# A four-layer graph kernel: TensorE's instructions in the last pipeline pinned to the order of the text, with a new order of the steps

## The chip, the cores and the metric

The kernel runs on one core of one Trainium2 chip. A core has five engines with a queue each: TensorE (PE in the profile, with its weight loads shown apart as PEld), VectorE (DVE), ScalarE (ACT), GpSimd (POOL) and SyncE (SP), which here only issues DMA transfers. Each takes its instructions in the order of its own list and waits for the others through semaphores. Every result of TensorE lands in PSUM, a small memory, and has to be read out by VectorE or ScalarE before that piece of PSUM can be written again.

The metric is the time of one execution in microseconds (us) on the device; the comparison uses the median over several executions.

## The reference

Sixteen graphs (B = 16) of 1024 nodes (N) with 128 features (D), fp32, and a 0/1 adjacency matrix for each. Four layers, each added to its input and normalised over the features. Cut to what matters:

```python
# layer 0: two batch norms over ALL graphs, so nothing behind them can start before every graph was read
w = masked_row_softmax(adj.T);  region = BN((w @ x) @ k1 + b1)
people = BN((w.T @ region) @ k2 + b2);  x = layernorm(x + people)
# layer 1: one score per node; softmax over axis 1 of the matrix
h = x @ W + b;  e = leaky(s1[:, None] + s2[None, :])       # s1 = h @ a1, s2 = h @ a2 + b_a
att = softmax(where(adj > 0, e, -9e15), axis=1);  x = layernorm(x + relu(att @ h))
# layers 2 and 3: scores are symmetric; only a_0 matters where adj is 0 or 1
s = leaky((x * a) @ x.T);  att = softmax(where(adj == 1, s, -9e15), axis=-1)
x = layernorm(x + att @ x)
```

## The kernel before

`fast_path` has two parts. The first (layer 0, up to about 384 us of the profile) streams all adjacency matrices once and builds the batch-norm sums; the change leaves it as it is. The second, from about 384 us on, is a software pipeline over the 16 graphs and holds all that is changed. C = 8 is the number of blocks of 128 nodes, H = 2 that of halves of 512, G = 2 that of groups of four blocks, A = 129 is D with a column of ones added, which gives the sums of the softmax.

For each graph b the class `Batch` holds the steps:

- residual 0: `load` (x and the saved layer-0 rows `people`, DMAs), `people_rows(g)` (four transposes on TensorE, L777, copied out by ScalarE), `add_people(g)` (four matmuls, L784; VectorE adds, L786 and L789, and collects layer-norm statistics, L722 and L723), then `Norm.apply`.
- layer 1: `transpose(g)` (L757), `scores1` (two matmuls, L804, and four exponentials on ScalarE into `u1`, `u2`), `values1` (eight matmuls, L816, read out by VectorE into `hn`, and the exponential `q`, L821), then `chunk1(c)` for eight chunks: loads of a strip of both matrices (L826, L834), the mask on ScalarE (L828), a check of symmetry on VectorE (L836), the weights `e1` in two passes on VectorE (L839, L842, some 1.2 us each), a reciprocal (L845), a scaling of `hn` on ScalarE (L846) and the two matmuls into `po` (L849). After chunk 7, `relu1` (ScalarE), `add_transposed(g)` (transposes L730) and `apply`.
- layers 2 and 3, the same code twice: `transpose(g)` with a copy and a scaled copy on ScalarE (L759, L761); `weights(c)`, a triangular strip of scores (matmuls into `pbig`, L869; VectorE L871 reads it out less the mask, L874 is the leaky slope; ScalarE L875 the exponential); `mirror(c)`, which transposes a strip's blocks into the other half of the matrix (L882, copied by ScalarE L884); `sum(c0, n)`, n times eight matmuls of 129 columns into `pacc` (L892), then VectorE's division and residual (L896 to L900) with statistics; `apply`; in layer 3 `store`.

`Norm.apply` is a short chain over three engines: GpSimd's power (L442, L443), one small VectorE instruction (L740) and eight ScalarE instructions, one for each block (L742).

fp32 matmuls appear in the trace as two records each; transposes as one.

What sets the order. The function builds a list of (time, step) pairs, sorts it, and calls the steps in that order; this is the order of the text. A "turn" is a unit of 1.0 of that time: one graph enters per turn, and each turn works on layer 1 of graph t, on layer 2 of t-1, and on layer 3 of t-2 and t-3. The steps of a stage are spread evenly between a start a and an end z:

```python
place(t, 0.04, 0.92, t, layer1)
place(t, 0.06, 0.44, t - 1, scores, 2, V_L2)
place(t, 0.56, 0.94, t - 1, sums_of, 2)
```

The text is not what runs. The kernel is written in a tile framework whose scheduler simulates the engines at build time and takes, for each engine, the ready instruction of the highest rank; so an instruction of the text can be moved before others on its own engine. It also allots the buffers: `ps_big` and `ps_acc` have three PSUM buffers each (`pbig`, `pacc`), `ps_sum` one (`po`); the loads of `adjt` and the weights `e1` have three buffers, those of `adjn` two, and `hn`, `u1`, `xt` and `e` one each.

Of the kernel before, what the change touches and what calls it, by code (L numbers as in the profile page):

```python
# [8 lines left out]
F32 = mybir.dt.float32  # L9
# [381 lines left out]
def fast_path(ctx, tc, x, adj, adjt, k1, k2, w1, vecs, b_w, b_a, out, bad):  # L391
# [312 lines left out]
    with tc.tile_pool(name="r_load", bufs=3) as loads, tc.tile_pool(name="r_rows", bufs=2) as rows, \  # L704
# [4 lines left out]

        class Norm:  # L710
# [14 lines left out]
            def add_transposed(self, src, xin, g):  # L725

                pt = ps_acc.tile([P, 4, P], F32, name="pacc")
                for k in range(4):
                    c = 4 * g + k
                    nc.tensor.transpose(pt[:, k, :], src[:, c * P:(c + 1) * P], ident)  # L730
                nc.vector.tensor_add(self.xl[:, 4 * g:4 * g + 4, :D], pt,
                                     xin[:, 4 * g:4 * g + 4, :D])
                for k in range(4):
                    self.collect(4 * g + k)
# [10 lines left out]
        class Batch:  # L745
            def __init__(self, b):
                self.b = b

            def transpose(self, xl, g, layer, by=None):

                if g == 0:
                    self.xt = work.tile([P, N], F32, name=f"xt{layer}_")
                    if by is not None:
                        self.xw = work.tile([P, N], F32, name=f"xw{layer}_")
                pt = ps_acc.tile([P, 512], F32, name="pacc")
                for k in range(4):
                    nc.tensor.transpose(pt[:, k * P:(k + 1) * P], xl[:, 4 * g + k, :D], ident)  # L757
                cols = slice(g * 512, (g + 1) * 512)
                nc.scalar.copy(self.xt[:, cols], pt)  # L759
                if by is not None:  # L760
                    nc.scalar.mul(self.xw[:, cols], pt, by)  # L761
# [12 lines left out]
            def people_rows(self, g):  # L774
                pt = ps_acc.tile([P, 512], F32, name="pacc")
                for k in range(4):
                    nc.tensor.transpose(pt[:, k * P:(k + 1) * P], self.g[:, 4 * g + k, :D], ident)  # L777
                nc.scalar.copy(self.gt[:, g * 512:(g + 1) * 512], pt)

            def add_people(self, g):  # L780
                pt = ps_acc.tile([P, 4, P], F32, name="pacc")
                for k in range(4):
                    c = 4 * g + k
                    nc.tensor.matmul(pt[:, k, :], self.gt[:, c * P:(c + 1) * P], wide["k12s"],  # L784
                                     start=True, stop=True)
                    nc.vector.scalar_tensor_tensor(self.x0[:, c, :], wide["c12s"],  # L786
                                                   self.g[:, c, D:A], self.x0[:, c, :], ALU.mult,
                                                   ALU.add)
                nc.vector.tensor_add(self.n0.xl[:, 4 * g:4 * g + 4, :D], pt,  # L789
                                     self.x0[:, 4 * g:4 * g + 4, :])  # L790
                for k in range(4):
                    self.n0.collect(4 * g + k)
# [4 lines left out]
            def scores1(self):  # L797
# [3 lines left out]
                for h in range(H):  # L801
                    cols = slice(h * 512, (h + 1) * 512)
                    pu = ps_big.tile([P, 512], F32, name="pbig")
                    nc.tensor.matmul(pu, wa1_rep, self.xt[:, cols], start=True, stop=True)  # L804
# [4 lines left out]
            def values1(self):  # L809
                self.hn = work.tile([P, C, A], F32, name="hn")  # L810
                for c0 in range(0, C, 3):
                    n = min(3, C - c0)
                    ph = ps_acc.tile([P, 3, A], F32, name="pacc")
                    for k in range(n):
                        c = c0 + k
                        nc.tensor.matmul(ph[:, k, :], self.xt[:, c * P:(c + 1) * P], w1_sb,  # L816
                                         start=True, stop=True)
# [4 lines left out]
                self.po = ps_sum.tile([P, N], F32, name="po")  # L822

            def chunk1(self, c):
# [10 lines left out]
                e = loads.tile([P, N], F32, name="e1")  # L835
# [10 lines left out]
                nc.scalar.mul(self.hn[:, c, :D], self.hn[:, c, :D], rs)  # L846
                for h in range(H):
                    cols = slice(h * 512, (h + 1) * 512)
                    nc.tensor.matmul(self.po[:, cols], self.hn[:, c, :D], e[:, cols],  # L849
# [12 lines left out]
            def weights(self, c, layer, v0):  # L862
                if c == 0:
                    self.e = work.tile([P, C, N], F32, name=f"e{layer}_")
                for a in range(c * P, N, 512):
# [3 lines left out]
                    nc.tensor.matmul(ps[:, :n], self.xw[:, c * P:(c + 1) * P], self.xt[:, cols],  # L869
# [7 lines left out]
            def mirror(self, c):  # L877
                for a in range(c + 1, C, 4):
                    n = min(4, C - a)
                    pt = ps_acc.tile([P, 4, P], F32, name="pacc")  # L880
                    for k in range(n):
                        nc.tensor.transpose(pt[:, k, :], self.e[:, c, (a + k) * P:(a + k + 1) * P],  # L882
                                            ident)
                    nc.scalar.copy(self.e[:, a:a + n, c * P:(c + 1) * P], pt[:, :n, :])  # L884

            def sum(self, c0, n, xl, layer):
                norm = self.norm
                po = ps_acc.tile([P, 3, A], F32, name="pacc")
                for k in range(n):
                    c = c0 + k  # L890
                    for m in range(C):
                        nc.tensor.matmul(po[:, k, :], self.e[:, m, c * P:(c + 1) * P], xl[:, m, :],  # L892
# [15 lines left out]
        def does(f, *a):  # L908
            return lambda: f(*a)

        def residual0(s):
            return [s.load, *[does(s.people_rows, g) for g in range(G)],
                    *[does(s.add_people, g) for g in range(G)],
                    lambda: s.n0.apply()]

        def layer1(s):
            return [*[lambda g=g: s.transpose(s.n0.xl, g, 1) for g in range(G)],
                    s.scores1, s.values1, *[does(s.chunk1, c) for c in range(C)], s.relu1,
                    *[lambda g=g: s.n1.add_transposed(s.ot, s.n0.xl, g) for g in range(G)],
                    lambda: s.n1.apply()]  # L920

        def scores(s, layer, v0):
            def begin():
                s.xin = s.n1.xl if layer == 2 else s.norm.xl
            return [begin, *[lambda g=g: s.transpose(s.xin, g, layer, vec[:, v0:v0 + 1])
                             for g in range(G)],
                    *[does(s.weights, c, layer, v0) for c in range(C)]]

        def mirrors(s):
            return [does(s.mirror, c) for c in range(C - 1)]  # L930

        def sums_of(s, layer):
            def begin():
                s.norm = Norm(layer)
            return [begin, *[lambda c=c: s.sum(c, min(3, C - c), s.xin, layer)
                             for c in range(0, C, 3)],
                    lambda: s.norm.apply()] + ([s.store] if layer == 3 else [])

        at_work = {}
        order = []  # L940

        def place(t, a, z, b, steps, *args):

            if 0 <= b < B:
                s = steps(at_work.setdefault(b, Batch(b)), *args)
                order.extend((t + a + (z - a) * k / len(s), f) for k, f in enumerate(s))


        for t in range(-1, B + 3):
            place(t, 0.04, 0.92, t, layer1)  # L950
            place(t, 0.06, 0.44, t - 1, scores, 2, V_L2)
            place(t, 0.24, 0.52, t - 1, mirrors)
            place(t, 0.56, 0.94, t - 1, sums_of, 2)
            place(t, 0.56, 0.94, t - 2, scores, 3, V_L3)
            place(t, 0.74, 1.02, t - 2, mirrors)
            place(t, 0.06, 0.44, t - 3, sums_of, 3)
            place(t, 0.30, 0.80, t + 1, residual0)
# [28 lines left out]
        nc.tensor.matmul(pt[:, :1], ones, count, start=True, stop=True)  # L986
# [51 lines left out]
```

## Time and profile before

| | |
|---|---|
| median of 4 runs | 1936.48 us (1935.09 to 1944.55) |
| the profiled execution, own time | 1937.93 us |
| its span, first to last instruction | 1936.1 us |
| mean granted TensorE clock | 0.924 of full |
| layer 0 and its moments | up to about 384 us |
| pipeline, first steady mark to last (twelve turns) | 601.92 to 1718.12 us, 93.0 us a turn |

How to read the profile. "Busy" is the time in which an engine has an instruction in work; the ends of matmuls are modelled. "Granted clock" is the share of its full clock that TensorE was given. In the timeline a row gives start, duration, engine, line of the code, operation, output and inputs and how many alike were merged; in square brackets stands the idle time of the engine ahead of it and the instruction that ended it. The steady marks of the table are the sums of layer 3 behind the transposes L757 in the chain of waits: they come back every 92.6 to 93.5 us.

### The profile page before, as it was taken

Reading aid. Unit: us, or ns where it says so; the run is one execution under the profiler, and the core shown is the slowest. Engines: PE = TensorE matmul, PEld = TensorE weight load, DVE = VectorE, ACT = ScalarE, POOL = GpSimd, SP = SyncE. Lnnn points to the kernel's source line nnn. Section 1 sums busy time; section 2 is a strip of 40 time slices with the busy share of each in tenths; the row PEclk is TensorE's granted clock in tenths of the full one; section 3 lists DMA queues with packets and bytes.
Section 4 is the critical chain, followed back from the end, with each engine's and each line's share of the span. In section 5 each row is a group of like instructions: output and inputs, shape, how many; then the busy total and the mean of one; then the engine's idle time right before and its main releaser. Section 6 shows DMA issues by size and latency. Waiting matters only on the chain.

```text
span 1936.1 us, 28354 instructions
## 1 busy us (share of the span) xinstructions
PE 1630.3 (84%) x10093; PEld 1298.4 (67%) x10093; DVE 1322.1 (68%) x3931; ACT 1027.5 (53%) x2161; POOL 137.1 (7%) x252
## 2 busy tenths in 40 slices
PE   6998999767888889797888888888888888888795
PEld 6988898734556666566666666666666657666684
DVE  4655555467796959595868777686868595958444
ACT  4534444236555555656565655556565555655533
POOL 0000000010100010110101010101000000000100
PEclk9999999869898989998989999898999898989888
DMA  8966664343350504041413232231414040402000
GB/s 295 321 238 248 242 223 159 107 143 91 122 158 8 163 12 158 21 148 34 136 51 119 72 98 92 78 110 59 136 34 149 20 157 13 147 1 74 11 1 25
DMA packets 110969, 216.53 MB, mean 112 GB/s; under 512 B 7776, under 2 KB 63712, under 8 KB 110816
## 3 DMA queue, kind: packets, MB, share of 16 engines
q1 hardware_dynamic: 108512, 206.08, 32.4%
q10 hardware_dynamic: 2304, 8.52, 1.1%
q8 instruction: 82, 1.34, 0.3%
q14 instruction: 71, 0.58, 0.1%
HBM read 197.67 MB, written 16.91 MB: 111 GB/s over the span
## 4 chain that ended last, share of the span: by engine, by line
PE 58%; DVE 14%; ACT 13%; DMA 9%; POOL 3%; issue 2%; SPq 0%; DVEq 0%; ACTq 0%
PE pacc L892 21%; PE pbig L869 8%; PE po L849 8%; PE pb L543 5%; DMA at<-in_adj_dram 5%; PE pz L506 4%; DMA adjt<-in_adjt_dram 3%; PE pacc L757 3%; PE pacc L882 2%; DVE e L839 2%; PE pbig L804 2%; PE pacc L816 1%; DVE ln_st L722 1%; ACT m L499 1%; ACT pen L828 1%
## 5 line engine op out<-in xcount | busy, mean ns | idle before, releaser
L849 PE MATMUL po<-e,hn 128*128 128x512 f32 x512 | 270.6, 661 | 78.2 <-ACT hn L846 77.8
L849 PEld LDWEIGHTS po<-e,hn 128*128 128x128 f32 x512 | 97.5, 207 | 190.1 <-ACT hn L846 108.8
L896 DVE TENSOR_SCALAR sums<-pacc 128x3 f32<-128x3 f32 (+1 forms) x96 | 15.4, 160 | 283.7 <-PE pacc L892 283.4
L543 PE MATMUL pb<-v,m 128*128 128x258 f32 x1024 | 156.0, 294 | 22.2 <-DVE g L548 21.9
L506 PE MATMUL pz<-x,m 128*128 128x258 f32 x1024 | 163.1, 301 | 7.0 <-ACT m L499 3.2
L828 ACT ACTIVATE pen<-adjt,minus_root 128x1024 fp8e5<-128x1024 int32 x128 | 147.2, 1150 | 38.9 <-DMA adjt<-in_adjt_dram 38.6
L839 DVE SCALAR_TENSOR_TENSOR e<-u,q,u 128x1024 f32<-128x1024 f32 x128 | 162.4, 1279 | 0.8 <-ACT q L821 0.8
L543 PEld LDWEIGHTS pb<-v,m 128*128 128x128 f32 x1024 | 137.9, 197 | 26.8 <-DVE g L548 24.3
L842 DVE SCALAR_TENSOR_TENSOR e<-e,adjt 128x1024 f32<-128x1024 f32 x128 | 154.8, 1220 | 0.0
L506 PEld LDWEIGHTS pz<-x,m 128*128 128x128 f32 x1024 | 139.9, 199 | 10.3 <-ACT m L499 4.7
L836 DVE SCALAR_TENSOR_TENSOR e<-adjn,adjt 128x1024 f32<-128x1024 int32 (+7 forms) x128 | 95.6, 749 | 14.4 <-PE po L849 12.6
L846 ACT ACTIVATE hn<-hn,rs 128x128 f32<-128x128 f32 x128 | 50.8, 402 | 80.3 <-DVE rs L845 75.8
L499 ACT CAST m<-at 128x1024 fp32r<-128x1024 int32 x64 | 66.0, 1048 | 44.3 <-DMA at<-in_adj_dram 44.3
L548 DVE TENSOR_TENSOR g<-pb,lo 128x129 f32<-128x129 f32 x128 | 36.0, 289 | 72.2 <-ACT lo L547 72.0
L509 DVE TENSOR_TENSOR z<-pz,lo 128x128 f32<-128x128 f32 x128 | 35.7, 288 | 66.4 <-ACT lo L508 66.1
L547 ACT COPY lo<-pb 128x129 f32<-128x129 f32 x128 | 33.1, 269 | 69.4 <-PE pb L543 67.4
L508 ACT COPY lo<-pz 128x129 f32<-128x129 f32 x128 | 33.1, 269 | 66.0 <-PE pz L506 65.8
L501 DVE CAST m<-at 128x1024 fp32r<-128x1024 int32 x64 | 44.1, 689 | 21.2 <-DMA at<-in_adj_dram 21.0
L536 PE MATMUL moments<-reg 128*128 128x130 f32 x256 | 48.6, 277 | 0.0
L551 PE MATMUL moments<-g 128*128 128x130 f32 x256 | 48.4, 274 | 0.0
L786 DVE SCALAR_TENSOR_TENSOR x<-c12s,g,x 128x128 f32<-128x128 f32 x128 | 39.0, 343 | 0.1
L551 PEld LDWEIGHTS moments<-g 128*128 128x128 f32 x256 | 39.0, 190 | 0.0
(1265 smaller groups left out, 4020.7 us busy)
## 6 DMA issues: line engine op xcount, KB each, us to landing
at<-in_adj_dram SPq DMA_DIRECT2D x128, 512.0 KB, 5.6
adjt<-in_adjt_dram SPq DMA_DIRECT2D x128, 512.0 KB, 4.2
people<-g ACTq DMA_DIRECT2D x16, 520.0 KB, 7.3
g<-people SPq DMA_DIRECT2D x16, 520.0 KB, 3.6
xf<-in_x_dram SPq DMA_DIRECT2D x16, 512.0 KB, 4.3
adjn<-in_adj_dram SPq DMA_DIRECT2D x16, 512.0 KB, 4.7
x<-in_x_dram SPq DMA_DIRECT2D x16, 512.0 KB, 5.5
adjn<-in_adj_dram SPq DMA_DIRECT2D x16, 448.0 KB, 4.7
```

Of the source, the lines that this page charges most:

```text
L499: nc.scalar.copy(self.m[:, i, :], at)
L506: nc.tensor.matmul(pz[:, :2 * A], self.m[:, i, c * P:(c + 1) * P], self.x2[:, i, :], start=(i == 0), stop=(i == C - 1))
L543: nc.tensor.matmul(pz[:, :2 * A], self.m[:, j, c * P:(c + 1) * P], self.v2[:, j].rearrange("p s a -> p (s a)"), start=(j == 0), stop=(j == ...
L551: nc.tensor.matmul(moments2[:, :A + 1], self.g[:, c, :D], self.g[:, c, :], start=(self.b == 0 and c == 0), stop=(self.b == B - 1 and c == ...
L757: nc.tensor.transpose(pt[:, k * P:(k + 1) * P], xl[:, 4 * g + k, :D], ident)
L828: nc.scalar.activation(self.pen[:, c, :], at, AF.Square, bias=minus_root, scale=BIG_ROOT, saturate=False, accum_out=checks[:, self.b, c:c ...
L836: nc.vector.scalar_tensor_tensor(e[:, :n], an[:, :n], 1.0, at[:, c * P:], ALU.mult, ALU.not_equal, accum_out=unlike[:, self.b, c:c + 1])
L839: nc.vector.scalar_tensor_tensor(e, self.u2, self.q[:, c:c + 1], self.u1, ALU.mult, ALU.max)
L842: nc.vector.scalar_tensor_tensor(e, e, 1.0, at, ALU.mult, ALU.mult, accum_out=total)
L849: nc.tensor.matmul(self.po[:, cols], self.hn[:, c, :D], e[:, cols], start=(c == 0), stop=(c == C - 1))
L869: nc.tensor.matmul(ps[:, :n], self.xw[:, c * P:(c + 1) * P], self.xt[:, cols], start=True, stop=True)
L892: nc.tensor.matmul(po[:, k, :], self.e[:, m, c * P:(c + 1) * P], xl[:, m, :], start=(m == 0), stop=(m == C - 1))
```

## The change

Three things, all in the pipeline and its `Norm`.

1. Every matmul and transpose of the pipeline goes through a small wrapper that calls `tc.keep_in_program_order`: the scheduler may not move it ahead of the TensorE instruction that stands before it in the text. The other engines' instructions are still ordered by the scheduler.
2. `chunk1` is cut in two: `weights1(c)` (loads, mask, weights, scaling of `hn`) and `sum1(c)` (the two matmuls into `po`), so that they can stand at different places of the text. `po` is allotted at the first sum instead of in `values1`.
3. The list of times is rewritten for each step by hand, with `weights1` of chunk c at 0.12 + 0.095 c and its `sum1` at 0.21 + 0.095 c of the turn, `mirror` about 0.11 behind the strip it reads, the sums of layers 2 and 3 at 0.44, 0.55 and 0.66 behind that layer's start, and so on.

No arithmetic is added or removed, and no buffer count changes.

```diff
+        def matmul(*args, **kwargs):
+            tc.keep_in_program_order(nc.tensor.matmul(*args, **kwargs))
+
+        def transpose(*args):
+            tc.keep_in_program_order(nc.tensor.transpose(*args))
...
-            def transpose(self, xl, g, layer, by=None):
+                self.e1 = {}
+
+            def transposed(self, xl, g, layer, by=None):
...
-                self.po = ps_sum.tile([P, N], F32, name="po")
-
-            def chunk1(self, c):
+
+            def weights1(self, c):
...
-                e = loads.tile([P, N], F32, name="e1")
+                e = self.e1[c] = loads.tile([P, N], F32, name="e1")
...
+
+            def sum1(self, c):
+                if c == 0:
+                    self.po = ps_sum.tile([P, N], F32, name="po")
                 for h in range(H):
                     cols = slice(h * 512, (h + 1) * 512)
-                    nc.tensor.matmul(self.po[:, cols], self.hn[:, c, :D], e[:, cols],
+                    matmul(self.po[:, cols], self.hn[:, c, :D], self.e1[c][:, cols],
                                      start=(c == 0), stop=(c == C - 1))
...
-        for t in range(-1, B + 3):
-            place(t, 0.04, 0.92, t, layer1)
-            place(t, 0.06, 0.44, t - 1, scores, 2, V_L2)
-            place(t, 0.24, 0.52, t - 1, mirrors)
-            place(t, 0.56, 0.94, t - 1, sums_of, 2)
-            place(t, 0.56, 0.94, t - 2, scores, 3, V_L3)
-            place(t, 0.74, 1.02, t - 2, mirrors)
-            place(t, 0.06, 0.44, t - 3, sums_of, 3)
-            place(t, 0.30, 0.80, t + 1, residual0)
+        for b in range(B):
+            s = Batch(b)
+            place(b - 0.80, s.load)
+            for g in range(G):
+                place(b - 0.68 + 0.02 * g, s.people_rows, g)
+                place(b - 0.60 + 0.03 * g, s.add_people, g)
+                place(b + 0.02 + 0.02 * g, lambda s=s, g=g: s.transposed(s.n0.xl, g, 1))
+                place(b + 0.94 + 0.02 * g,
+                      lambda s=s, g=g: s.n1.add_transposed(s.ot, s.n0.xl, g))
+            place(b - 0.54, lambda s=s: s.n0.apply())
+            place(b + 0.07, s.scores1)
+            place(b + 0.09, s.values1)
+            for c in range(C):
+                place(b + 0.12 + 0.095 * c, s.weights1, c)
+                place(b + 0.21 + 0.095 * c, s.sum1, c)
+            place(b + 0.90, s.relu1)
+            place(b + 0.97, lambda s=s: s.n1.apply())
+            for layer, v0, at in ((2, V_L2, b + 1.08), (3, V_L3, b + 2.53)):
+                place(at, norm_of, s, layer)
+                for g in range(G):
+                    place(at + 0.01 + 0.02 * g,
+                          lambda s=s, g=g, l=layer, v=v0: s.transposed(s.xin, g, l, vec[:, v:v + 1]))
+                for c in range(C):
+                    place(at + 0.06 + 0.035 * c, s.weights, c, layer, v0)
+                for c in range(C - 1):
+                    place(at + 0.17 + 0.04 * c, s.mirror, c)
+                for k, c in enumerate(range(0, C, 3)):
+                    place(at + 0.44 + 0.11 * k,
+                          lambda s=s, c=c, l=layer: s.sum(c, min(3, C - c), s.xin, l))
+                place(at + 0.75, lambda s=s: s.norm.apply())
+            place(b + 3.35, s.store)
```

In the built program the TensorE lists differ as the change says. Before, the eight `po` pairs of a turn stand close together, the fourth to the sixth with one or two other rows of the list between them; after, they stand five to twelve rows apart over the whole turn. The lists of VectorE and ScalarE, which the scheduler makes, differ too.

## The prediction

> **What bounds the kernel now.** I read the page first, then the windows of a steady turn, then TensorE's timeline of that turn and its clock.
>
> ```profile
> PE 1630.3 (84%) x10093; PEld 1298.4 (67%) x10093; DVE 1322.1 (68%) x3931; ACT 1027.5 (53%) x2161; POOL 137.1 (7%) x252
> ...
> PE 58%; DVE 14%; ACT 13%; DMA 9%; POOL 3%; issue 2%; SPq 0%; DVEq 0%; ACTq 0%
> ```
>
> The second line is the chain of waits by engine: TensorE leads, but over 40% of the span the chain runs elsewhere. The turn from 830 us, all engines (PE, PEld, DVE, ACT, POOL, then clock, DMA share, GB/s):
>
> ```profile
> 830.00:923.00 93.00, 79.40 (x469) 60.65 (x468) 68.72 (x208) 53.57 (x110) 7.98 (x12) 0.93 0.28 89
> ```
>
> TensorE is idle for 13.6 of 93.0 us, VectorE for 24.3. TensorE's timeline shows where:
>
> ```profile
> 871.70 0.44 PE L882 MATMUL pacc<-ident,e__8094 128*128 128x128 f32 x2 [2.91 <-ACT e__8094 L875]
> 877.48 0.48 PE L882 MATMUL pacc<-ident,e__8094 128*128 128x128 f32 x1 [5.34 <-ACT e__8094 L875]
> ...
> 880.31 6.85 PE L892 MATMUL pacc<-xl__7201,e__8094 128*128 128x129 f32 x48
> ...
> 890.98 5.52 PE L892 MATMUL pacc<-xl__7201,e__8094 128*128 128x129 f32 x48
> ...
> 916.70 3.32 PE L849 MATMUL po<-e,hn 128*128 128x512 f32 x4 [4.51 <-ACT hn L846]
> ...
> 921.19 1.88 PE L849 MATMUL po<-e,hn 128*128 128x512 f32 x4
> ```
>
> Three gaps (2.91, 5.34, 4.51) make 12.8 of the 13.6 us. The reader should also see their echo: the same 48 sums take 6.85 us behind a gap and 5.52 later; the same two matmuls of `po` 3.32 and 1.88. The granted clock in windows of 2 us explains it:
>
> ```profile
> 876.00:878.00 2.00, 0.52 (x3) 0.50 0.00 0
> ...
> 880.00:882.00 2.00, 2.00 (x11) 0.50 0.04 8
> ```
>
> The clock is halved from about 877.5 to 883 and from 916.7 to 920.3, which costs half of 9.1 us, 4.5. So a turn is 93.0 = work at full clock + 13.6 + 4.5, the work being 74.9. From rows at full clock: sums 256 records at 0.112 (5.36 us for 48 from start to start) 28.6; `po` 32 at 0.43 13.8; scores 9216 columns in two passes at 0.43 for 512, 15.5; 96 transposes at 0.11, 10.6; L804, L816, L784 5.3. Sum 73.8; the missing 1.1 I keep as 1.5% of friction.
>
> The long gaps come from the layer norm, which ScalarE's queue puts ahead of exponentials TensorE needs:
>
> ```profile
> 870.11 0.20 POOL L442 TENSOR_SCALAR rs_t<-ln_mv__8116 128x8 f32<-128x8 f32 x1
> ...
> 870.39 1.81 POOL L443 TENSOR_TENSOR ln_rstd__8311<-rs_t,neg_half 128x8 f32<-128x8 f32 x1
> ...
> 873.86 3.17 ACT L742 ACTIVATE xl__8114<-xl__8114,ln_off__8315,ln_rstd__8311 128x128 f32<-128x128 f32 x8
> ```
>
> From VectorE's last statistic it takes 2.1 us on GpSimd, 0.2 on VectorE and 3.1 on ScalarE.
>
> **The change, part by part.** The wrapper and the split of `chunk1` add no instruction: their own cost is nothing, since the same 73.8 us of TensorE, 69 of VectorE and 54 of ScalarE remain. What they change is who stands ahead of whom, so I followed one turn of the new lists, engine by engine, with durations from rows. VectorE's rows overlap: an L839 at 902.77 lasts 1.28 but its successor starts at 903.96, so it counts 1.19. The clock starts with VectorE's first L839 of a graph, which waits for `q`.
>
> A. VectorE, up to the reciprocal of chunk 5. Now layer 2's strips stand between the chunks: seven L839 at 1.19 (8.3), six L842 at 1.22 (7.3), layer 2's L871 and L874 (4608 columns each at 0.60 for 512, 10.8), four L836 (2.4), L769 (1.2), two L789 (1.2), ten pairs of statistics (2.9), some twenty small ones (2.0). 36.1 us, and 1.6 of waiting for GpSimd in the norm of residual 0, which has 0.5 us of other VectorE work in front. TensorE has only 27.7 us of work in this stretch and loses ten us in gaps: 1.4 (`po` of chunk 1 for L846), 1.8 (a PSUM buffer that ScalarE reads late behind eight L742), 4.3, 1.7 and 0.8. The 4.3 is `po` of chunk 3: ScalarE has the mask L828 of another chunk ahead of its scaling L846, and that chunk's strip is loaded only when VectorE's L842 frees the buffer. SP's queue has the 520 KB of `people` just ahead of it; in the turn shown a strip issued at 924.33 reached its mask at 929.47, 5.1 us. Behind that `po` stand layer 2's sums, and for them waits the norm of layer 2. It ends at 37.7.
>
> B. Scaling of chunk 5 on ScalarE, and behind it the copies L759 and L761 of layer 3: 0.2 + 0.4 + 0.6 + 0.7. At 39.6 TensorE starts layer 3's scores.
>
> C. TensorE without a gap to the end of layer 2's last sum: 3840 columns of scores 6.4, two chunks of `po` 3.4, 80 records of sums 9.0, 13 transposes 1.4. 20.2, to 59.8. VectorE has 18 us in the stretch and keeps up.
>
> D. From that sum to the relu: VectorE's division and statistics 2.2, GpSimd 2.1, L740 0.2, then on ScalarE eight L742 (3.1), with three copies and two exponentials (2.0) ahead of the relu (0.6). 10.2, to 70.0. TensorE has 7 us of other work there and stands 2.9. What is late next are the transposes of the relu.
>
> E. From the relu to the copy of the next graph's layer-1 rows: transposes and L731 1.9, statistics 2.4, GpSimd 2.1, L740 0.2, eight L742 3.1, copy 0.6, in all 10.3, to 80.3. TensorE has 7.3 of sums and transposes and stands 3.0: this copy is behind the eight L742 in ScalarE's queue, though it does not need them.
>
> F. TensorE to the next graph's first strip: L804 1.7, 48 records of sums 5.4, transposes 0.9, L816 1.8, one L869 0.9, and 0.8 of waiting for ScalarE; `q` 0.2. 11.7, to 92.0.
>
> Sum: 36.1 + 1.6 + 1.9 + 20.2 + 10.2 + 10.3 + 11.7 = 92.0 at full clock. It leaves TensorE idle for 18 us (less its work of 73.8) instead of 13.6, with 4.3 instead of 5.34 as the largest gap.
>
> What this leaves out: friction of 1.5% on the 32 us of TensorE on the path, 0.5; VectorE's seams in A, where windows of 10 us filled by it show 9.7 busy, 0 to 1.1, taken 0.6; and the clock. For gaps near 3 us the nearest row is one at the pipeline's start:
>
> ```profile
> 428.00 2.74 PE L849 MATMUL po<-e,hn 128*128 128x512 f32 x4 [2.58 <-ACT hn L846]
> ```
>
> Those four records take 1.88 at full clock: 0.9 lost behind a gap of 2.58 us. So each of the gaps of 4.3, 2.9 and 3.0 may cost between 0 and the 2.7 us lost behind 5.34; behind the first, TensorE's 1.7 us of slack takes part; behind the second, the chain of E runs on other engines. I take 1.2, 0.3 and 0.2: 1.7 together, bounds 0 and 3.5.
>
> The Trainium skill, "TensorE: Matmul & The Clock Gate", Part 1, says the clock is halved after an idle window of about 3.4 us that runs freely, and advises no gaps above some 3 us. By that rule only the 4.3 us gap would cost anything and the clock term would be 1.2; by the row above, where 2.58 us were enough, it is the 1.7 I take.
>
> A turn is then 92.0 + 0.5 + 0.6 + 1.7 = 94.8 against 93.0, bounds 92.5 and 97.1. Thirteen such turns lie between the second and the fifteenth graph: 13 x 1.8 = 23 us. I cost the fill and the drain of the pipeline at nothing: at both ends there is little to interleave, and the chains (eight chunks of 3.7 us on VectorE at the start; scores, sums, norm of the last graph at the end) do not change; bounds -10 and +10. The profiled execution took 1937.93, so 1961; the median lies 1.5 below it: 1960.
>
> **The rivals.**
>
> Faster. The layer-1 chunks now spread over the turn, and VectorE's 24 idle us are there to be used. If the relu and the copy in D and E come before the L742 that I put ahead of them, TensorE has no gap after B: 39.6 + (73.8 - 27.7) = 85.7, with friction and seams 87. That is -6 a turn, 13 x -6 = -78, 1858. For it: a norm's eight L742 and TensorE's sums are of like length, so a us of error in the chain moves it. Against: ScalarE's list is fixed as I read it. It decides from the point where the two gaps in D and E, 5.9 us in my sum, fall under 3 together.
>
> Much slower. The load of part A is the rule, not one case: each strip waits for L842, the mask for the strip, and `po` for what stands behind the mask in ScalarE's queue; pinned, nothing passes it on TensorE. With two more gaps of 2 us on the path, 98.7 a turn: 13 x 5.7 = 74, 2010. For it: SP's list now mixes `people`, x and the strips. Against: ten turns of before show only 14 us of L828 waiting for its strip, and spreading the chunks gives the loads more time.
>
> Nothing to see. Gaps change places and the sum stays: 92.3 to 93.7 a turn, 1927 to 1946. That the pinning does nothing at all I exclude: the TensorE lists of the two programs differ.
>
> **How the numbers follow.** About 0.5% (10 us) is what a measurement of this kernel can tell; three of the four runs agree within 2 us, one lies 8 above. Forecast (93.7 to 97.5 a turn) 0.45, 1946 to 1995, likeliest 1960; much slower 0.15; nothing to see 0.12; faster 0.28. So slower 0.60, same 0.12, faster 0.28. The range leaves out half of the faster case and a third of the much slower one, together 0.19: 1885 to 2005.
>
> **What would show it.** In the profile of the changed kernel: a steady turn of 94 to 95 us; TensorE's busy time about unchanged, with more but shorter gaps; a gap of about 4 us at a `po` in the first half of a turn, ended by the scaling L846 that stands behind a mask in ScalarE's queue; gaps of about 3 us at the transposes of the relu and at the matmuls of `scores1`, both ended by ScalarE; the large VectorE wait of before (13.5 us for a sum) cut up. Wrong I am if a turn comes in below 92 us, and then the step to look at is D or E; if A runs longer than 39 us, the step is the loads.

## The result, and the profile after

| | before | after |
|---|---|---|
| median | 1937.98 us (1927.64 to 1944.75, 78 runs) | 1941.59 us (1929.34 to 1950.1, 52 runs) |
| ratio to before, 95% interval | | 1.002 (1.0011 to 1.0028) |
| profiled execution: span | 1936.1 us | 1942.2 us |
| of it, from the pipeline's first transposes to the end | 1545.9 us | 1547.8 us |
| steady turn, mean of eleven | 93.0 us | 92.9 us |
| mean granted clock | 0.924 | 0.942 |

The change makes the kernel 0.2% slower: the interval excludes 1, but the step is below the 0.5% that the prediction took as the least a measurement can tell. The steady turns are counted between the relu's transposes of the fourth and of the fifteenth graph. The fourth row counts from the transposes of `people` of the first graph, where the unchanged layer 0 ends. That point lay between 383.2 and 397.0 us in the fourteen profiled executions of this study, with the same code ahead of it, so profiles are compared from there.

In the lines of after the two wrapped calls have one line each, L713 for every matmul and L716 for every transpose; they are told apart by their tiles. L847 and L850 are the two passes of VectorE over the weights of layer 1, L854 ScalarE's scaling of `hn`, L836 the mask, L750 the layer norm's last pass, L768 and L770 the copies of transposed rows, L868 the relu, L887 the exponential, L896 the copy of a mirrored block.

The page of after: the engines' busy times, and the chain of waits by engine.

```profile
PE 1639.2 (84%) x10093; PEld 1302.9 (67%) x10093; DVE 1328.5 (68%) x3931; ACT 1021.0 (53%) x2161; POOL 152.7 (8%) x252
...
PE 46%; DVE 24%; ACT 13%; DMA 8%; POOL 6%; issue 2%; SPq 0%; DVEq 0%; ACTq 0%
```

The busy times are those of before within 1%, but for GpSimd's (152.7 us for 137.1). The chain has moved: VectorE has 24% of it instead of 14%, TensorE 46% instead of 58%. The same stretch of 93 us as before, by the windows view:

```profile
830.00:923.00 93.00, 79.41 (x468) 59.98 (x467) 69.70 (x209) 53.31 (x112) 9.19 (x12) 0.96 0.27 87
```

TensorE is idle for 13.6 us of it, to a tenth what it was. Where it stands idle is new. TensorE's timeline of after, one turn:

```profile
838.55 3.19 PE L713 MATMUL po<-e,hn 128*128 128x512 f32 x4 [3.80 <-ACT hn L854]
841.53 6.05 PE L713 MATMUL pacc<-xl__7512,e__7721 128*128 128x129 f32 x48
...
849.28 1.98 PE L713 MATMUL pbig<-xt__8048,xw__8049 128*128 128x512 f32 x4 [0.83 <-ACT xw__8049 L770]
...
876.95 0.33 PE L716 MATMUL pacc<-ident,e__8064 128*128 128x128 f32 x1 [0.89 <-ACT e__8064 L887]
879.91 1.78 PE L716 MATMUL pacc<-ident,u 128*128 128x128 f32 x8 [2.62 <-ACT u L868]
881.48 6.53 PE L713 MATMUL pacc<-xl__6890,e__8064 128*128 128x129 f32 x48
...
890.53 1.98 PE L713 MATMUL pbig<-xt__8390,wa_rep 128*128 128x512 f32 x4 [1.65 <-ACT xt__8390 L768]
```

The gaps of 5.34 and 2.91 us at the mirror transposes are gone. In their place stand 3.80 at the `po` pair of chunk 3, 2.62 at the transposes of the relu, 1.65 at `scores1` and several smaller ones, all ended by ScalarE. The echo of the slow clock is still there: the pair of `po` 3.19 us, the 48 sums behind it 6.05, and 6.53 behind the relu.

ScalarE's timeline of after shows why chunk 3's `po` is late:

```profile
836.96 1.15 ACT L836 ACTIVATE pen<-adjt,minus_root 128x1024 fp8e5<-128x1024 int32 x1 [1.91 <-DMA adjt<-in_adjt_dram]
...
838.11 0.39 ACT L854 ACTIVATE hn<-hn,rs 128x128 f32<-128x128 f32 x1
```

The mask of another chunk waits 1.91 us for its strip, and the scaling that `po` needs stands behind it.

### The profile page after: what moved, and what is told of

It is laid out like the page before. It is cut to its first block, busy times and chain, and to the rows that moved or that the text cites. A ratio compares the mean times of both kernels' runs of the same rounds, so it can differ in the third digit from the quotient of the medians.

```text
span 1942.2 us, 28298 instructions
## 1 busy us (share of the span) xinstructions
PE 1639.2 (84%) x10093; PEld 1302.9 (67%) x10093; DVE 1328.5 (68%) x3931; ACT 1021.0 (53%) x2161; POOL 152.7 (8%) x252
## 4 chain that ended last, share of the span: by engine, by line
PE 46%; DVE 24%; ACT 13%; DMA 8%; POOL 6%; issue 2%; SPq 0%; DVEq 0%; ACTq 0%
PE pacc L713 18%; PE pbig L713 7%; PE pb L543 6%; PE po L713 5%; DMA at<-in_adj_dram 5%; DVE e L847 4%; PE pz L506 4%; PE pacc L716 4%; DVE e L850 4%; DMA adjt<-in_adjt_dram 2%; DVE ln_st L730 2%; POOL rs_t L442 1%; ACT m L499 1%; DVE e L844 1%; PE moments L536 1%
## 5 line engine op out<-in xcount | busy, mean ns | idle before, releaser
L713 PE MATMUL po<-e,hn 128*128 128x512 f32 x512 | 272.2, 659 | 82.9 <-ACT hn L854 82.9
L713 PEld LDWEIGHTS po<-e,hn 128*128 128x128 f32 x512 | 97.7, 204 | 175.3 <-ACT hn L854 96.4
L836 ACT ACTIVATE pen<-adjt,minus_root 128x1024 fp8e5<-128x1024 int32 x128 | 146.6, 1150 | 49.5 <-DMA adjt<-in_adjt_dram 48.8
L847 DVE SCALAR_TENSOR_TENSOR e<-u,q,u 128x1024 f32<-128x1024 f32 x128 | 163.6, 1279 | 9.6 <-ACT q L830 9.5
L850 DVE SCALAR_TENSOR_TENSOR e<-e,adjt 128x1024 f32<-128x1024 f32 x128 | 155.5, 1216 | 0.0
L908 DVE TENSOR_SCALAR sums<-pacc 128x3 f32<-128x3 f32 (+1 forms) x96 | 15.3, 159 | 201.6 <-PE pacc L713 200.6
L854 ACT ACTIVATE hn<-hn,rs 128x128 f32<-128x128 f32 x128 | 51.5, 403 | 106.1 <-DVE rs L853 106.0
L716 PE MATMUL pacc<-ident,u 128*128 128x128 f32 x128 | 27.7, 387 | 43.2 <-ACT u L868 43.2
L716 PEld LDWEIGHTS pacc<-ident,u 128*128 128x128 f32 x128 | 21.2, 196 | 47.9 <-ACT u L868 47.5
```

Of the source, the lines that this page charges most:

```text
L713: tc.keep_in_program_order(nc.tensor.matmul(*args, **kwargs))
L716: tc.keep_in_program_order(nc.tensor.transpose(*args))
L836: nc.scalar.activation(self.pen[:, c, :], at, AF.Square, bias=minus_root, scale=BIG_ROOT, saturate=False, accum_out=checks[:, self.b, c:c ...
L847: nc.vector.scalar_tensor_tensor(e, self.u2, self.q[:, c:c + 1], self.u1, ALU.mult, ALU.max)
L850: nc.vector.scalar_tensor_tensor(e, e, 1.0, at, ALU.mult, ALU.mult, accum_out=total)
```

## The experiments

Twelve kernels. All times of a row come from that kernel; the ratio is to before on the same chip. "Pipeline" and "turn" are the profiled execution's, counted as in the table above.

| kernel | ratio to before (95%) | pipeline, us | turn, us |
|---|---|---|---|
| before | 1 | 1545.9 | 93.0 |
| after | 1.002 (1.0011 to 1.0028) | 1547.8 | 92.9 |
| e1_pin_only: old text, pinned | 1.0584 (1.0554 to 1.0615) | 1656.5 | 100.2 |
| e2_order_only: new text, not pinned | 0.9843 (0.9816 to 0.987) | 1517.9 | 91.7 |
| e3_warm | 0.9984 (0.9967 to 1.0001) | 1543.1 | 92.5 |
| e9_warm_both | 1.0301 (1.0268 to 1.0333) | 1599.6 | 96.8 |
| e12_warm_big | 1.0013 (0.9993 to 1.0033) | 1544.4 | 92.4 |
| e6_apply_late | 0.9859 (0.9807 to 0.9911) | 1518.3 | 91.4 |
| e7_sum_later | 0.9828 (0.977 to 0.9886) | 1508.4 | 90.2 |
| e4_early_layer1 | 0.9595 (0.9573 to 0.9618) | 1464.0 | 87.4 |
| e5_early_unpinned | 0.9452 (0.9405 to 0.9499) | 1430.2 | 85.1 |
| e8_both_moves | 0.9411 (0.9361 to 0.9461) | 1437.1 | 85.6 |
| e11_moves_later | 0.9748 (0.9706 to 0.9791) | 1492.4 | 89.3 |
| e10_moves_unpinned | 0.9155 (0.9114 to 0.9196) | 1386.2 | 82.1 |

### The two halves of the change

e1 puts the wrapper into the kernel before and leaves its text alone; e2 takes it out of the changed kernel.

```diff
 # e1, in the kernel before
-    nc.tensor.transpose(pt[:, k, :], ...)
+    transpose(pt[:, k, :], ...)          # and so for all matmuls of the pipeline
 # e2, in the changed kernel
-    tc.keep_in_program_order(nc.tensor.matmul(*args, **kwargs))
+    nc.tensor.matmul(*args, **kwargs)    # and so for transpose
```

> The kernel before, its order of the text untouched, with TensorE's instructions of the pipeline pinned to it; nothing else of the change. Theory W (a turn is the chain that I walked: VectorE's, ScalarE's and GpSimd's queues in series with stretches of TensorE; TensorE's own gaps and its slow clock lie beside it) has the sums of a chunk directly behind the chunk's weights in this text, so pinned TensorE waits for the whole of each chunk with everything else behind it: slower, 97 to 102 us a turn, 1990 to 2055. Rival N (pinning and placing both do next to nothing, and the result near zero is the sum of two nothings): 1930 to 1948.

> The changed kernel with the pinning taken away: the same steps at the same places of the text, TensorE's instructions free again for the scheduler. Theory W: the scheduler brings TensorE's work ahead where it finds it ready, the chain over VectorE's waits for q stays, 92 to 94 us a turn, 1925 to 1950. Rival G (pinning costs and the new places gain, and they cancelled): under 1915 here, as much faster as the pinning alone is slower. Rival N: 1930 to 1948.

Measured: the pin alone costs 5.8%, the new text alone wins 1.6%. In pipeline us the pin costs 111 with the old text and 30 with the new one; the text wins 28 without the pin and 109 with it. The result of 0.2% is thus no sign of a change that does little. Its two halves are each large enough to be measured, and cancel.

What the pin costs is work that stands behind a waiting instruction. Over the whole run TensorE is idle for 166.2 us ahead of `po` in e1, and for 78.2 in before. TensorE's timeline of e1 (the wrapper's lines are L711 and L714 there, the scaling L852, the mirror copy L881):

```profile
1423.73 0.47 PE L714 MATMUL pacc<-ident,e__12004 128*128 128x128 f32 x1 [5.34 <-ACT e__12004 L881]
...
1453.08 2.84 PE L711 MATMUL po<-e,hn 128*128 128x512 f32 x4 [2.24 <-ACT hn L852]
...
1463.93 3.44 PE L711 MATMUL po<-e,hn 128*128 128x512 f32 x4 [4.57 <-ACT hn L852]
```

The gap of 5.34 us at a mirror transpose stayed, and in this turn four `po` pairs wait, of which these are two; before had one such wait a turn, 4.51 us. TensorE's timeline of e2 at the place where after loses 3.80 us:

```profile
905.64 2.69 PE L713 MATMUL pacc<-xl__8294,e__8503 128*128 128x129 f32 x22 [0.84 <-ACT e__8503 L896]
908.17 1.88 PE L713 MATMUL po<-e,hn 128*128 128x512 f32 x4
909.89 3.06 PE L713 MATMUL pacc<-xl__8294,e__8503 128*128 128x129 f32 x26
```

The scheduler has put 22 sums of layer 2 ahead of that `po` pair, which then waits for nothing. A wait of 2.45 us stands ahead of the next pair, that of chunk 4, where after has none. The groups of the page give the whole run: matmuls into `po` and their idle time ahead (last column), of after,

```profile
L713 PE MATMUL po<-e,hn 128*128 128x512 f32 x512 | 272.2, 659 | 82.9 <-ACT hn L854 82.9
```

and of e2:

```profile
L713 PE MATMUL po<-e,hn 128*128 128x512 f32 x512 | 273.5, 662 | 43.0 <-ACT hn L854 43.0
```

### The slow clock

Idle matmuls of `ident` and `ones`, whose result nobody reads, fill gaps so that the clock is not halved behind them. They add work to TensorE and change nothing else.

```diff
 # e3, in sum1, ahead of the matmuls of chunk 3
+    if c == 3:
+        warm = ps_acc.tile([P, 512], F32, name="pacc")
+        for k in range(14):
+            matmul(warm[:, :P], ident, ones, start=True, stop=True)
 # e9: e3, and in add_transposed, ahead of the relu's transposes
+    if g == 0:
+        warm = ps_acc.tile([P, 512], F32, name="pacc")
+        for k in range(10):
+            matmul(warm[:, :P], ident, ones, start=True, stop=True)
 # e12: as e9, but eight pairs, into a buffer of pbig
+        warm = ps_big.tile([P, 512], F32, name="pbig")
```

> The changed kernel with 14 matmuls of a constant (128 columns, two records each, some 3.1 us at full clock, written to a PSUM buffer that nobody reads) ahead of the po matmuls of chunk 3, in the gap of 3.8 us that ends there. They keep TensorE busy, so that the po of chunk 3 and the 48 sums behind it run at full clock (1.9 and 5.4 us instead of 3.2 and 6.0). Theory W: the slow clock behind that gap lies beside VectorE's chain, the turn stays at 93.0 within 0.4 and the time within 5 us of the changed kernel's. Rival C (the slow clock lies on the path, as I had it in my sum): 1.2 to 2 us a turn less, 16 to 26 us faster than the changed kernel.

> e3_warm with ten more idle matmul pairs of ident and ones ahead of the relu's transposes, so that both gaps behind which the changed kernel's TensorE runs at half clock are filled. My forecast counted 1.7 us a turn for the slow clock. Theory W (the slow stretch ahead of the next gap lies beside ScalarE's chain): nothing more than e3_warm gave, turn 92.0 to 92.4, 1925 to 1936. Rival C (the slow clock behind the relu's gap sits on the path, 1 to 1.5 us): turn 90.8 to 91.4, 1910 to 1922.

> e9_warm_both put right: eight idle matmul pairs ahead of the relu's transposes that write a tile of the other ring (pbig), whose buffers are free there, so that they run in the gap and don't wait for a copy of ScalarE's as those of e9 did. Theory W (the slow clock behind the relu's gap lies beside ScalarE's chain, and only the gap ahead of scores1 grows by it): as e3_warm, turn 92.0 to 92.4, 1925 to 1936. Rival C (it is on the path, 1 to 1.5 us a turn): turn 90.8 to 91.4, 1910 to 1922.

Measured: e3 takes 0.4 us off a turn and 5 off the pipeline, between the two theories. e9 misfired: its turn is 4.4 us longer than that of e3. TensorE's timeline of e9 (in e9 and e12 the lines of the kernel are four or eight numbers higher: L772 is the copy of the rows, L876 the relu, L904 the mirror copy):

```profile
985.23 4.13 PE L713 MATMUL pacc<-ones,ident 128*128 128x128 f32 x20 [1.86 <-ACT e__9017 L904]
989.16 1.07 PE L716 MATMUL pacc<-ident,u 128*128 128x128 f32 x8
```

The idle matmuls first waited 1.86 us for a buffer that a ScalarE copy still read, then ran 4.13 us, and the relu's transposes started at 989.16, 6.12 us behind the mirror transpose of 983.04; in after that distance is 2.96. So e9 says nothing on the clock. It does show that the relu's transposes lie on the path: 3.2 us later there, 4.4 us more a turn. e12 puts it right. Its timeline, the lines that answer to after's, and the next turn's behind them:

```profile
871.43 1.95 PE L713 MATMUL pbig<-ones,ident 128*128 128x128 f32 x16
874.22 1.14 PE L716 MATMUL pacc<-ident,u 128*128 128x128 f32 x8 [0.84 <-ACT u L876]
875.19 5.52 PE L713 MATMUL pacc<-xl__6986,e__8199 128*128 128x129 f32 x48
884.32 3.38 PE L713 MATMUL pbig<-xt__8534,wa_rep 128*128 128x512 f32 x4 [2.73 <-ACT xt__8534 L772]
...
967.31 1.14 PE L716 MATMUL pacc<-ident,u 128*128 128x128 f32 x8 [0.84 <-ACT u L876]
977.41 1.98 PE L713 MATMUL pbig<-xt__9340,wa_rep 128*128 128x512 f32 x4 [2.73 <-ACT xt__9340 L772]
...
1059.03 1.14 PE L716 MATMUL pacc<-ident,u 128*128 128x128 f32 x8 [0.84 <-ACT u L876]
```

The transposes take 1.14 instead of 1.78 us and the sums 5.52 instead of 6.53, and the gap ahead of `scores1` is 2.73 instead of 1.65. In the first of these turns the clock is slow behind that gap instead (3.38 for 1.98), in the second it is not. From relu to relu they take 93.1 and 91.7 us: the slow `scores1` costs its whole 1.4. Of the eleven turns seven take 91.7, without a slow stretch. Two take 93.1, slow at `scores1`, and one 96.4, slow there for twice as long and again at the scores of layer 3. The last, near the drain, takes 92.2. So the mean, that of e3 to 0.1 us, hides what a full clock is worth: the fills move the slow stretch in some turns to places where it costs more. The executions of e12 say the same: the fastest had 1928.66 us at a mean clock of 0.970, the slowest 1942.26 at 0.961.

e3 shows what the slow stretch behind the relu's gap costs. Two turns that follow each other, TensorE's timeline of e3:

```profile
1241.65 1.14 PE L716 MATMUL pacc<-ident,u 128*128 128x128 f32 x8 [2.62 <-ACT u L872]
1242.62 7.17 PE L713 MATMUL pacc<-xl__10138,e__11342 128*128 128x129 f32 x48
...
1251.75 1.98 PE L713 MATMUL pbig<-xt__11668,wa_rep 128*128 128x512 f32 x4 [1.09 <-ACT xt__11668 L768]
...
1333.34 1.97 PE L716 MATMUL pacc<-ident,u 128*128 128x128 f32 x8 [2.62 <-ACT u L872]
...
1344.17 1.98 PE L713 MATMUL pbig<-xt__12465,wa_rep 128*128 128x512 f32 x4 [0.95 <-ACT xt__12465 L768]
```

In the first turn the transposes ran at full clock and the sums behind them lost 1.6 us (7.17 for 5.52); `scores1` starts 10.10 us behind the transposes, as at full clock, and the turn is 91.7. In the second the transposes were slow too (1.97 for 1.14); `scores1` starts 10.83 us behind them and the turn is 92.4, as eight of e3's eleven are. So neither theory holds whole. The slow sums lie beside ScalarE's chain and cost nothing, as theory W says; the slow transposes lie on it and cost 0.7 us a turn.

But for the idle matmuls, TensorE's list in e3 and e12 is that of after, instruction by instruction; in e12's steady turns ScalarE's is the same too, and VectorE's but for one exchange of two small instructions a turn. So 91.7 us is after's turn at full clock, and its slow clock costs 1.2 of its 92.9. The two fills together win back 0.5 of that; by the ratios e12 (1.0013) can't be told from after (1.002).

### The layer norm ahead of the relu

```diff
-    place(at + 0.75, lambda s=s: s.norm.apply())
+    place(at + (0.83 if layer == 2 else 0.75), lambda s=s: s.norm.apply())
```

> The changed kernel with one line of text moved: layer 2's closing ScalarE pass (L750, eight of 0.3 us) at 0.83 instead of 0.75 of its layer, behind the relu of the next graph in the text. By my prediction's step D the relu stands behind those eight, and TensorE's gap of 2.62 us ahead of L716 on u comes from it. Theory D: the gap goes down by the some 1.5 to 2 us of the passes that the relu no longer stands behind, the turn 93.1 to 91 to 91.8; 13 turns less some 17 to 27: 1915 to 1925. Rival (the relu has waited for its last po sum all along, or the gap moves on to scores1): no change, 1935 to 1945.

Measured: turn 91.4, median 1908.55 us, somewhat below theory D's 1915 to 1925; that the relu stands behind the norm's passes, step D of the prediction, is confirmed. TensorE's timeline of e6:

```profile
960.37 1.41 PE L716 MATMUL pacc<-ident,u 128*128 128x128 f32 x8 [0.83 <-ACT u L868]
...
970.63 1.99 PE L713 MATMUL pbig<-xt__9172,wa_rep 128*128 128x512 f32 x4 [2.26 <-ACT xt__9172 L768]
```

The relu's gap falls from 2.62 to 0.83, and of these 1.8 us 0.6 come back at `scores1` (2.26 for 1.65).

### The sums of layer 1 later in the text

```diff
-    place(b + 0.90, s.relu1)
+    place(b + 0.915, s.relu1)
-    place(b + 0.21 + 0.095 * c, s.sum1, c)
+    place(b + 0.245 + 0.095 * c, s.sum1, c)
```

> The changed kernel, still pinned, with the sums of layer 1 placed 0.035 of a turn later in the text (0.245 instead of 0.21, relu 0.915 instead of 0.90). The 4th po pair then stands behind 24 sums of layer 2, which were ready. Theory H (what the pin loses is the work that stands behind a po pair that waits): the 3.80-us gap closes, and the turn falls from 93.1 to 89.5 to 91.5; 1895 to 1925, about what the unpinned e2_order_only has. Rival V (VectorE's row of layer-1 weights sets when the po sums end, and so the relu; moving the sums only moves the gap): gap found elsewhere, 1935 to 1955.

Measured: 0.9828 and a turn of 90.2, pinned, about what e2 has without the pin; idle time ahead of `po` falls from 82.9 to 19.8 us. Theory H is borne out here: in after the pin costs because the text puts a `po` pair ahead of work that is ready. The slow clock shows here as well: four of the eleven turns, with a slow stretch of 6.8 us around the 4.21-us gap named next, take 91.9 to 92.6 us, and three with none until their last 1.3 us take 88.4. Part of the gain goes back into a gap of 4.21 us at a mirror transpose that now waits for ScalarE.

### Layer 1 begun early

```diff
-    place(b + 0.02 + 0.02 * g, lambda s=s, g=g: s.transposed(s.n0.xl, g, 1))
+    place(b - 0.16 + 0.02 * g, lambda s=s, g=g: s.transposed(s.n0.xl, g, 1))
-    place(b + 0.07, s.scores1)
-    place(b + 0.09, s.values1)
+    place(b - 0.035, s.scores1)
+    place(b - 0.034, s.values1)
```

> The changed kernel with the next graph's layer-1 start moved ahead of the sums of layer 3 in the text: its transposes from 0.02 to -0.16, scores1 and values1 from 0.07 and 0.09 to -0.035 and -0.034 of the turn. The work is the same. Theory W: the 48 sums, the eight L742 of layer 1 and the copies leave the way between the relu and q, VectorE begins the next graph's chunks some 16 us earlier, and the scores of layer 2 start 3 to 4 us earlier with two chunks already done: 83 to 87 us a turn, 1835 to 1885. Rival T (the pinned TensorE list with its PSUM buffers sets the turn, and moving work within it changes nothing): 1930 to 1950.

> The early layer 1 of e4_early_layer1 with the wrapper that keeps TensorE's order taken out. Theory H (the pin costs because layer 1's sums, waiting for VectorE and ScalarE, hold back ready work behind them): in e4 only 18.8 us of po gaps are left in the whole run (82.9 in the changed kernel), so there is little to win; 1840 to 1865, within 1% of e4. Rival K (the pin costs a fixed 2%, wherever things stand): 36 us less than e4, about 1821. Rival S (without the pin the scheduler brings the early work back to where it was): near e2_order_only, 1890 to 1905.

> e4_early_layer1 with layer 2's closing ScalarE pass moved as in e6_apply_late. Theory D: the gaps of ScalarE's order that are left in e4 (two of 2.5 us at pbig behind L770) shrink, turn 88 to 86 to 87.3, 1830 to 1850. Rival (with layer 1 early, the relu is no longer on the path): 1852 to 1862, no change.

Measured: e4 wins 4%, the turn falls to 87.4. The copy of the next graph's rows no longer stands behind the norm of the one before, nor the start of its layer 1 behind 48 sums of layer 3; which of the two gave more was not taken apart. And in the stretch from 900 to 995 us TensorE has no gap ahead of `scores1`. e8, with the norm moved as well, has 85.6 and 1821.59 us, better than theory D's 86 to 87.3 and 1830 to 1850, but not where it said: the two gaps at `pbig` are still 2.50 and 2.12 us (2.50 and 1.79 in e4). What is gone is 0.3 of the relu's gap (0.91 to 0.59) and a gap of 1.10 at a mirror transpose; with the 0.3 by which one of the two grew, that is 1.1 of the 1.9 us won, and the rest was not traced. e5 takes the pin out of e4 and wins more than theory H allowed (1827.69 us against 1840 to 1865), less than rival K's 1821; neither hit.

### Both moves, without the pin, or with a still later text

```diff
 # e10: e8 with the wrapper's pin taken out, as in e2
 # e11: e8 with the sums and relu of e7, and
-    place(at + 0.06 + 0.035 * c, s.weights, c, layer, v0)
+    place(at + 0.08 + 0.035 * c, s.weights, c, layer, v0)
```

> e8_both_moves with the wrapper that pins TensorE taken out. Theory H (the pin costs the ready work that stands behind whichever instruction waits; in e8 that is two gaps of 2.5 us ahead of the strips of layers 2 and 3, at most 5 us a turn, of which e5 won 2.4): turn 85.6 to 83 to 84.3, 1790 to 1810. Rival (the turn is by now set by VectorE's and ScalarE's chain and the gaps are slack): 1815 to 1825.

> e8_both_moves, still pinned, with layer 1's sums 0.035 later, its relu 0.015 later (as in e7_sum_later) and the strips of layers 2 and 3 placed 0.02 later in the text, so that less stands behind the two waits of 2.5 us. Theory H: text alone does what the scheduler does, near e10_moves_unpinned, 1790 to 1812. Rival (a later text delays what hangs on the strips, mirrors and sums): 1820 to 1840.

Measured: e10 is the fastest kernel of the study, 1775.94 us, ratio 0.9155, and beats before and after. It gained more than theory H said (85.56 to 82.13, 3.4 us a turn, where 1.3 to 2.6 were expected). Two lines of TensorE's timeline, of e8:

```profile
901.31 3.15 PE L713 MATMUL pbig<-xt__8830,xw__8831 128*128 128x512 f32 x4 [2.50 <-ACT xw__8831 L770]
...
951.47 3.49 PE L713 MATMUL pbig<-xt__9256,xw__9257 128*128 128x512 f32 x8 [2.12 <-ACT xw__9257 L770]
```

and of e10:

```profile
928.26 2.84 PE L713 MATMUL pbig<-xt__9256,xw__9257 128*128 128x512 f32 x6 [0.84 <-ACT xw__9257 L770]
...
962.91 1.98 PE L713 MATMUL pbig<-xt__9612,xw__9613 128*128 128x512 f32 x4 [1.06 <-ACT xw__9613 L770]
```

The gaps ahead of the strips fall from 2.50 to 1.06 and from 2.12 to 0.84, and the four matmuls behind the first run in 1.98 us instead of 3.15. That would be 2.7 us of gaps and 1.2 of slow clock, 3.9 in all against 3.4 measured, and other gaps changed too. The turns without any slow stretch tell the two apart better: the one that e8 has among its eleven took 83.4 us, the five of e10 80.8 to 82.2, 81.3 in the mean. So some 2.1 us came from the order, within what theory H said, and the rest from fewer slow stretches, which my expectation had left out. The windows view of e10: TensorE is busy for 85.8 of 93 us and VectorE for 75.8.

```profile
900.00:993.00 93.00, 85.84 (x515) 64.65 (x514) 75.83 (x228) 60.85 (x129) 10.45 (x15) 0.98 0.30 92
```

e11 came out at 1885.8 us, 74 above theory H's upper end and 46 above the rival's: a later text is no substitute for the scheduler in general. The strips that it moves are what the mirror transposes need, and TensorE now waits there, timeline of e11:

```profile
899.87 0.76 PE L716 MATMUL pacc<-ident,e__8503 128*128 128x128 f32 x5 [2.94 <-ACT e__8503 L896]
```

e11 moved three things at once; which of them costs most was not taken apart.

## Why the prediction was wrong

The forecast was a clear loss of 23 us; it is 4 by the medians. The clock of the walk starts with VectorE's first L847 of a graph, at 808.84 in the turn shown. "At full clock" is the turn of 91.7 us that e12 has seven times; its marks agree within 0.03 us from turn to turn.

- A and B, to the first scores of layer 3: 39.6 said, 40.4 found (849.28), 39.4 at full clock. The place and the cause of the largest gap were right too: 4.3 said and 3.80 found, with the mask ahead of the scaling and the strip late. VectorE waited 2.7 us for GpSimd (0.88 and 1.81) where I had 1.6.
- C, to the last sum of layer 2: 59.8 said; the last sums end at 869.6, 60.8; 59.7 at full clock.
- D, to the relu: 70.0 said; its transposes start at 879.91, 71.1; 70.0 at full clock. e6 shows that the norm's passes ahead of the relu are what holds it.
- E, to the copy of the next graph's rows: 80.3 said; `scores1` starts at 890.53, 81.7; 80.1 at full clock. e4, which takes that copy out from behind the norm and the next graph's start out from behind the sums of layer 3, has a turn 5.5 us shorter.
- F, to the next graph's first L847: 92.0 said; it comes at 902.17, 93.3; 91.7 at full clock. The mean turn is 92.9.
- **The step that failed** is what I added to this walk: friction 0.5, VectorE's seams 0.6 and the slow clock 1.7, 2.8 us a turn, times thirteen. 0.9 is left in the mean turn. The mechanism was right, the sizes were not. The larger error is friction and seams: 1.1 said, and at full clock nothing is left of it, for the turn is 0.3 below the walk at 91.7. The walk's durations, taken from start to start of rows, must have held it already. The clock term was 0.5 too large, 1.2 instead of 1.7, and its places were about right: on the mean of eleven turns some 0.9 us are lost up to the first scores of layer 3, where I had 1.2, and some 0.4 from the relu's transposes to `scores1`, where I had 0.3; at `scores1`, where I had 0.2, after's clock is full. In the turn shown the stretches behind 3.80 and 2.62 us together ran 3.4 us over their times in e12 (3.19 for 1.98, 6.05 for 5.53, 1.78 for 1.14, 6.53 for 5.52), and the turn was 1.6 longer than at full clock. The other 1.8 us came out of TensorE's next gaps: 0.83 instead of 2.13, 1.65 instead of 2.73.
- Fill and drain: costed at nothing. The pipeline is 1.9 us longer while eleven turns are 0.8 shorter, so 2.7 us for both ends, within the bounds of 10. The rest of the 6 us between the two spans lies ahead of the pipeline.
- TensorE's idle time: 18 us a turn said, 13.6 found. TensorE was busy for 79.4 us, not 73.8: 3.4 of the difference is the slow clock, and the other 2.2 is busy time that my sum of rows did not hold.
- VectorE's wait for the sums was to be cut up: it was, the idle time ahead of L908 (L896 before) falls from 283.7 to 201.6 us, by the groups of the two pages.

The rivals. "Nothing to see" (92.3 to 93.7 a turn, 1927 to 1946) is what happened, with 92.9 and 1941.59, and I had given it 0.12. That the two kernels come out so close is luck: e1 and e2 show two effects that cancel. I had found a walk of 92.0 against 93.0 and then let small additions, each on the slow side, decide the sign. "Faster" needs D and E to go; they did not by themselves, but e8 (85.6 a turn) shows that moving them in the text gives what that rival worked out, 87 and less. "Much slower": strips do come late (ScalarE's 1.91 us above), but only inside a gap that A had counted. More buffers for the strips were not tried. That the pin and the text are two changes of opposite sign I did not say at all; I had priced the wrapper at nothing, and e1 and e2 show it at 111 and 30 us. It was in the walk unseen, since the walk followed the pinned lists.

Open: how much of the 30 to 51 us that the pin costs in the other kernels (e4 to e5, after to e2, e8 to e10) belongs to each gap; only the two gaps of e8 were traced.

## What to carry to other kernels

Where durations are taken from start to start of rows, as in this walk, do not add friction on top: at full clock it was right within 0.3 of 92 us. A slow clock counts only where the chain runs through that engine: the slow sums cost nothing here, the slow transposes 0.7 us and the slow `scores1` 1.4. Look at single turns by their clock before believing a mean. Test a pinned order and a new text apart: the pin cost time in all four pairs here. If an instruction that waits has ready work behind it in the text, move it back or let the scheduler do so; but e11 shows that a later text can cost more than it wins. A few moved lines of the schedule, which change what stands ahead of what in ScalarE's queue and in TensorE's, were worth 6% against the kernel before with the pin, and 8% without.

## What the runs showed of the hardware

The clock of after in windows of 2 us, TensorE only (busy, clock, DMA share, GB/s):

```profile
838.00:840.00 2.00, 1.45 (x3) 0.80 0.84 250
840.00:842.00 2.00, 2.00 (x6) 0.50 0.78 288
...
880.00:882.00 2.00, 2.00 (x11) 0.54 0.00 0
882.00:884.00 2.00, 2.00 (x13) 0.61 0.00 0
```

By the trace's own record of the clock it is half from 839.19 to 842.60 us and from 880.15 to 883.56. All its changes lie on a grid of 3.41 us, in this trace and in the thirteen others; two of the eleven turns have two such stretches in a row behind the `po` gap. The length of a gap alone does not decide it. In e4, four matmuls behind a gap of 2.50 us took 1.98 (904.26) and the same four of the next graph behind 2.48 us took 3.62 (988.99); a gap of 2.83 us in e7 left the transposes at 1.14. What does is how long TensorE was busy in the window before: 0.57 us from 876.73 to 880.15. In after's pipeline the clock was halved behind windows with up to 1.53 us of work and stayed full behind windows from 1.46 us on; in the fourteen traces the border lies between 1.4 and 2.2 us, by the profile's modelled ends.

The Trainium skill, "TensorE: Matmul & The Clock Gate", Part 1, speaks of a window of about 3.4 us that runs freely, which agrees with the grid of 3.41 us and with the same gap costing at one time and not at another. But it asks for a whole idle window, and here a window with up to 1.53 us of work in it was enough.
